# Selective scan of a two-layer vision block: two product buffers, one broadcast bank, two shared banks, and a hand-fixed VectorE order

## The chip, the cores and the metric

The kernel runs on one core of one Trainium2 chip. The metric is the device time of one execution in microseconds (us); of the kernel before there are three runs, and their median is the time to compare with. A core has five engines with an instruction stream each: TensorE (PE, matrix products; PEld is its weight load), VectorE (DVE), ScalarE (ACT), GpSimd (POOL) and SyncE (SP, which issues the DMAs here). Each engine works through its own stream in order, and waits on semaphores where it needs another engine's result. SBUF is the working memory, PSUM the memory that TensorE writes to.

## What is computed

The input is an image batch of 2 x 96 channels x 96 x 96. Two layers follow each other, each with a convolution-like part and a quantised feed-forward part. Only the first part of layer 0 matters here. Cut down, it is:

```python
xin, z = split(einsum(x, in_proj_w))            # 192 channels each; z = silu(z)
x_s    = grid_sample(xin, offsets(conv3x3(xin)))
# 6x6 = 36 tokens per sequence, 4 scan orders (rows, columns, both reversed)
x_dbl  = einsum(xs4, x_proj_weight)             # -> dts, Bs, Cs
delta  = softplus(dts + bias)
def step(h, (u, dt, b, c)):                     # 16 states per channel
    dA = exp(dt * A)
    h  = h * dA + (dt * u) * b                  # the scan
    y  = einsum(h, c)
y = sum of the four orders + D*u -> layer norm -> * z -> out_proj
```

So each of 192 channels has 16 states and four scan orders, and each state is a first-order recurrence along 36 tokens: `h = h * dA + (dt*u*b)`.

## The kernel before

**Tiling.** Layer 0 is cut into 32 stripes (2 images x 16 stripes of 6 rows, 576 tokens). Each stripe has three parts: a front (`_l0_front`: norm, projection, 3x3 convolution, sampling, B, C and the step sizes, stored to DRAM), the scan (`_l0_scan`) and a back (`_l0_back`: norm, gate, output projection, feed-forward). The front of stripe n+1 and the back of stripe n-1 run beside the scan of stripe n.

**A unit.** The scan of a stripe is 64 units: two halves `h` of the channels (32 units each), two token orders `o`, two directions `kk`, four quarters `i` of the states, two token halves `c`. One unit covers 128 partitions (32 channels x 4 states) and 3 blocks x 288 tokens = 864 elements. I count units from 0 to 63 within a stripe, and write for unit u:

- B(u): TensorE broadcasts the token's B to the partitions with one matmul into a PSUM bank (`spread`, L1040)
- p(u): VectorE multiplies it with `dur` into the PSUM tile `bp` (`product`, L1045; `bp` takes two banks)
- s(u): VectorE's scan from `dA` and `bp` into the SBUF tile `h` (L1060)
- t(u): GpSimd multiplies `h` with C in place (`times_c`, L1065)
- y(u): TensorE sums the states into the PSUM bank `y` (`states`, L1077); after it the `h` tile is free

`dA` is made on ScalarE, three instructions for two units (L1025), into two buffers; so the decay of units 2q and 2q+1 waits until s(2q-3) has read its buffer. There are six `h` tiles (`P.nh`). At the start of each half, six pairs of matmuls (`direct`, L966 and L968) put the D term into the bank `y`; they wait until ScalarE has copied the half before out of it (`out`, L976 and L978). `out` writes the tile `Y`, of which there is one: the next stripe's first half can leave only when the back of this one has read `Y` (its projection `pp`, L932 and L935, after GpSimd's gate, L921).

**PSUM.** Its 8 banks are dealt out as `y` one, `B` two, `bp` one tile of two banks, and three banks of the tag `p`, which all matmuls of the fronts and backs share.

**What sets the order.** The operations of all stripes are collected in a planner (`_Plan`). Each has an engine, a cost in us, tiles read and written and a due time. `order` simulates the engines: it starts next what can start first, and among what can start at once what is due first; across engines it adds a delay (`LAG`). A tile takes a slot of its tag when its first operation starts. The order found is then fixed for each engine, SP too (`_in_order`). The planner reckons with its own costs; the chip keeps the order, and waits where it must.

**Waits put ahead.** `wait` in `product` hangs extra waits on the products with c == 0: for the decays of this unit, and for t and y of unit u-5, if these were issued by then. The scan then has fewer waits of its own.

Of the kernel before, what the change touches and what calls it, by code (L numbers as in the profile page):

```python
# [13 lines left out]
ALU = mybir.AluOpType  # L14
# [14 lines left out]
WIN = 6  # L29
# [3 lines left out]
H2 = T // 2  # L33
NS = 16
KG = 4
NQ = 4
CB = 32
NBL = C // CB
# [50 lines left out]
class _Op:  # L89
    def __init__(self, eng, cost, run, due, tab):  # L90
        self.eng, self.cost, self.run, self.due, self.tab = eng, cost, run, due, tab
        self.deps, self.tiles, self.start, self.end = set(), [], None, None
        self.left, self.then, self.ready = 0, [], 0.0

SAME = 0.06
LAG = {"pe": 0.5, "dve": 1.5, "act": 0.6, "pool": 1.0, "sp": 1.5}


class _Plan:
# [39 lines left out]
    def order(self):  # L142

        free = {e: 0.0 for e in ("pe", "dve", "act", "pool", "sp")}
        ready = {e: [] for e in free}
        tab, wire = None, 0.0
        for n, o in enumerate(self.ops):
            o.no = n
            o.left = len(o.deps)
            for p in o.deps:  # L150
                p.then.append(o)
        for o in self.ops:
            if not o.left:
                ready[o.eng].append(o)
        left, out = {id(t): len(t.users) for o in self.ops for t in o.tiles}, []
        while len(out) < len(self.ops):
            best = None
            for e, queue in ready.items():
                pick = None
                for o in queue:  # L160
                    at = max(free[e], o.ready)
                    for t in o.tiles:
                        if t.slot is None:
                            s = t.place()
                            if s is None:
                                at = None
                                break
                            at = max(at, s[1] + (SAME if s[2] == e else LAG[e]))
                    if at is None:
                        continue  # L170
                    worth = o.due
                    if o.tab is not None and o.tab != tab:
                        worth += 5.0

                    key = (max(at, free[e] + 0.1), worth, o.no)
                    if pick is None or key < pick[0]:
                        pick = (key, at, o)
                if pick and (best is None or pick[1] < best[1]):
                    best = pick
            assert best, "the plan is stuck"  # L180
            _, at, o = best
            ready[o.eng].remove(o)
            cost = o.cost
            if o.tab is not None and o.tab != tab:
                tab, cost = o.tab, cost + 1.3
            for t in o.tiles:
                if t.slot is None:
                    t.slot = t.place()
                    t.slot[0] = t
                    if t.tag != "p":  # L190
                        t.queue.pop(0)
            o.start = at
            if o.eng == "sp":
                free["sp"] = at + 0.6
                wire = max(wire, at + 1.0) + cost
                o.end = wire + 2.0
            else:
                o.end = free[o.eng] = at + cost
            for p in o.then:
                p.left -= 1  # L200
                p.ready = max(p.ready, o.end + (SAME if p.eng == o.eng else LAG[p.eng]))
                if not p.left:
                    ready[p.eng].append(p)
            for t in o.tiles:
                left[id(t)] -= 1
                if o.end > t.slot[1]:
                    t.slot[1:] = o.end, o.eng
                if not left[id(t)]:
                    t.slot[0] = None
            out.append(o)  # L210
        return sorted(out, key=lambda o: (o.start, o.no))
# [739 lines left out]
def _l0_scan(k, P, S, n, f, tau):  # L951


    nc = k.nc
    f.Y = S.tile(P.hand, [C, 2, T], "Y", 1)
    for h in range(2):

        py = S.tile(P.ps, [128, 512], "y", 1)
        t0 = (64 * n + 32 * h) * tau

        def direct(h=h, py=py):

            for b in range(NBL):
                w = k.w_D[:, h, b * CB : b * CB + CB]
                v = f.xs0.ap[:, h]
                nc.tensor.matmul(py.ap[b * CB : b * CB + CB, :HEAD], w, v[:, :HEAD],  # L966
                                 start=True, stop=False)
                nc.tensor.matmul(_tail(py, b), w, v[:, HEAD:], start=b == 0, stop=False)  # L968

        S.op("pe", 1.4, direct, (f.xs0,), (py,), due=t0)  # L970
        for o in range(2):
            for kk in range(2):
                _l0_section(k, P, S, f, 64 * n + 32 * h, o, h, kk, py, t0 + (16 * o + 8 * kk) * tau, tau)

        def out(h=h, py=py):
            nc.scalar.copy(f.Y.ap[:, h, :HEAD], py.ap[:C, :HEAD])  # L976
            for b in range(NBL):
                nc.scalar.copy(f.Y.ap[b * CB : b * CB + CB, h, HEAD:], _tail(py, b))  # L978

        S.op("act", 1.4, out, (py,), (f.Y,), due=t0 + 33 * tau)  # L980
# [5 lines left out]
def _tail(py, b):  # L986

    n = T - HEAD
    return py.ap[NBL * CB :, b * n : b * n + n]


def _l0_section(k, P, S, f, first, o, h, kk, py, at, tau):
# [40 lines left out]

    def unit(u, i, c, cre, dA, t0):
        toks = slice(c * H2, (c + 1) * H2)
        pB, bp = S.tile(P.ps, [128, 512], "B", 2), S.tile(P.ps, [128, 1024], "bp", 1)
        ht = S.tile(P.rep, [128, NBL, H2], "h", P.nh)

        def spread():
            nc.tensor.matmul(  # L1040
                pB.ap[:, :H2], k.selb[:, kk, i, :], f.bc[o].ap[:, toks], start=True, stop=True)
            P.issued["B", u] = latest()

        def product():
            nc.vector.tensor_tensor(  # L1045
                bp.ap[:, : NBL * H2].rearrange("p (b n) -> p b n", b=NBL), dur.ap[:, :, toks],
                pB.ap[:, :H2].unsqueeze(1).to_broadcast([128, NBL, H2]), ALU.mult)
            if c == 0:
                free = u + 1 - P.nh
                wait([("act", u), ("B", u + 1), ("pool", free), ("pe", free)])  # L1050

        S.op("pe", 0.3, spread, (f.bc[o],), (pB,), due=t0 - P.early["pe"] * tau)
        S.op("dve", 1.13, product, (dur, pB), (bp,), due=t0 - P.early["dve"] * tau)

        def scan():
            hv, dv = (v.rearrange("p b n -> p (b n)") for v in (ht.ap, dA.ap[:, c]))
            bv = bp.ap[:, : NBL * H2]
            if kk:
                hv, dv, bv = hv[:, ::-1], dv[:, ::-1], bv[:, ::-1]
            nc.vector.tensor_tensor_scan(hv, dv, bv, 0.0, ALU.mult, ALU.add)  # L1060

        S.op("dve", 2.0, scan, (dA, bp), (ht,), due=t0 + (1.35 - P.early["dve"]) * tau)

        def times_c():
            nc.gpsimd.tensor_tensor(  # L1065
                ht.ap, ht.ap, cre.ap[:, toks].unsqueeze(1).to_broadcast([128, NBL, H2]), ALU.mult)
            P.issued["pool", u] = latest()

        S.op("pool", 2.06, times_c, (cre,), (ht,), due=t0 + (2.3 - P.early["pool"]) * tau)

        def states():
            end = o == 1 and kk == 1 and i == NQ - 1

            def part(dst, v, stop):
                if o:
                    v = v.rearrange("p (w j i) -> p w i j", i=WIN, j=WIN)
                nc.tensor.matmul(dst, k.fold, v, start=False, stop=stop)  # L1077

            for blk in range(NBL):
                dst = py.ap[CB * blk : CB * blk + CB]  # L1080
                n = HEAD - H2 if c else H2
                part(dst[:, c * H2 : c * H2 + n], ht.ap[:, blk, :n], end and c == 1)
            if c:
                for blk in range(NBL):
                    part(_tail(py, blk), ht.ap[:, blk, n:], end and blk == NBL - 1)
            P.issued["pe", u] = latest()

        S.op("pe", 1.0, states, (ht,), (py,), due=t0 + (3.5 - P.early["pe"]) * tau)

    for i in range(NQ):  # L1090
        quarter(i)
# [2 lines left out]
def _layer0(k, tc, a, x, x2d):  # L1094
# [3 lines left out]
    with ExitStack() as st:  # L1098
# [10 lines left out]
        P.ps = pool("ps0", 1, space=PSUM)  # L1109
        P.tc, P.issued = tc, {}  # L1110
        P.early = {"pe": 60, "act": 60, "dve": -30, "pool": 0, "sp": 8}
        P.np, P.ng, P.nda, P.nh = 3, 5, 2, 6
        start = len(nc.cur_bb.bb.instructions)
        S, tau = _Plan(k), 3.4
        stripes = [(b, s) for b in range(NB) for s in range(NW)]
        F = [Ctx() for _ in stripes]

# [831 lines left out]
```

## Time and profile before

| | us |
|---|---|
| median of 3 runs (8774.3 to 8780.41) | 8775.34 |
| span of the profiled execution | 8782.9 |
| first product to last scan | 146.8 to 6730.3 |
| 64 units of one stripe, mean | 205.7 |
| VectorE busy in 3000 to 3200 us | 190.93 of 200 |
| GpSimd busy in the same stretch | 181.78 of 200 |
| ScalarE busy in the same stretch | 149.30 of 200 |

The page gives busy time by engine and by groups of instructions; each group's row ends with the idle time of its engine just before it and what ended most of that. The scan stage is the stretch from 147 to 6730 us; layer 1 takes the rest. In the scan stage, a unit costs 6583.5 / 2048 = 3.21 us, of which VectorE's two instructions take 1.061 + 1.953 us.

### The profile page before, as it was taken

The page shows a single profiled execution, that of the slowest core. Times are in us where ns is not written, and L with a number is a line of the kernel's source. Part 1 is how long each engine was busy: PE and PEld are TensorE (multiplying, and loading weights), DVE is VectorE, ACT ScalarE, POOL GpSimd, SP SyncE. Part 2 cuts the span into 40 slices and gives each one's busy share as a digit, 9 for nine tenths or more (in the row PEclk, how much of TensorE's full clock was granted, in tenths as well). Part 3 has the DMA queues.
Part 4 walks back from the last instruction along what each step waited for, and adds up shares of the span by engine and source line. Part 5 has one row for each costly group of instructions (what it writes and reads, how often), then busy time and mean ns, then how long its engine had stood idle before and what let it go on. Part 6 is the DMA issues. An engine that isn't in the chain of part 4 may idle for free. (4 is left out here: it accounts for less than half of the span.)

```text
span 8782.9 us, 119686 instructions
## 1 busy us (share of the span) xinstructions
PE 7366.0 (84%) x43653; PEld 3436.2 (39%) x43653; DVE 8004.4 (91%) x5398; ACT 6381.2 (73%) x10720; POOL 6026.5 (69%) x3835
## 2 busy tenths in 40 slices
PE   7888888888888888888888888888865999989998
PEld 4333434434434343343343434334422323542245
DVE  3899999999999999999999999999997898959988
ACT  5677777777777777777777777777764787678867
POOL 4999998988899899898998888898885000010001
PEclk8898888998988888898888889888866999989999
DMA  2444444444444444444444444444442000110001
GB/s 85 139 149 144 145 145 141 146 143 141 142 141 145 137 151 144 142 142 146 145 142 143 142 143 138 145 139 142 142 140 87 19 2 9 34 51 2 3 21 32
DMA packets 339996, 985.64 MB, mean 112 GB/s; under 512 B 50152, under 2 KB 51872, under 8 KB 339104
## 3 DMA queue, kind: packets, MB, share of 16 engines
q1 hardware_dynamic: 337488, 977.74, 35.4%
q8 instruction: 346, 5.67, 0.3%
q14 instruction: 258, 2.11, 0.1%
q10 hardware_dynamic: 1904, 0.12, 0.0%
HBM read 797.19 MB, written 139.25 MB: 107 GB/s over the span
## 5 line engine op out<-in xcount | busy, mean ns | idle before, releaser
L1065 POOL TENSOR_TENSOR h<-h,cre 128x864 f32<-128x864 f32 x2048 | 4124.1, 2023 | 692.6 <-DVE h L1060 493.1
L1060 DVE TENSOR_TENSOR_SCAN h<-dA,bp 128x864 f32<-128x864 f32 x2048 | 3999.8, 1953 | 84.7 <-PE y L1077 6.3
L1025 ACT ACTIVATE dA<-dlr,A 128x576 f32<-128x576 f32 x3072 | 2156.4, 765 | 1098.8 <-DVE h L1060 1015.1
L1045 DVE TENSOR_TENSOR bp<-dur,B 128x864 f32<-128x864 f32 x2048 | 2172.9, 1061 | 295.9 <-PE B L1040 48.7
L1077 PE MATMUL y<-h,fold 128*32 128x288 f32 (+2 forms) x18432 | 1870.7, 452 | 161.6 <-POOL h L1065 152.0
L1040 PE MATMUL B<-bt,selb 128*128 128x288 bf16 x2048 | 642.4, 315 | 963.5 <-DVE bp L1045 951.1
L551 PE MATMUL pc<-xin,off 96*96 96x288 f32 x4608 | 1321.4, 414 | 0.5 <-ACT xin L516 0.4
L1077 PEld LDWEIGHTS y<-h,fold 128*32 128x32 f32 x18432 | 764.3, 119 | 1138.1 <-issue 548.9
L1413 ACT ACTIVATE pr<-sc 128x960 f32<-128x960 f32 (+1 forms) x1080 | 954.1, 937 | 200.3 <-PE sc L1409 180.3
L1493 DVE TENSOR_TENSOR sums<-sums,pr 128x3840 f32<-128x3840 f32 (+1 forms) x240 | 959.1, 3996 | 55.2 <-ACT pr L1413 33.2
L551 PEld LDWEIGHTS pc<-xin,off 96*96 96x96 f32 x4608 | 708.3, 165 | 514.3 <-issue 268.4
L1585 POOL MEMSET vch<- 96x32 f32 x16 | 2.4, 153 | 1296.6 <-DVE dist L1447 1209.3
L1040 PEld LDWEIGHTS <-selb 128*128 128x128 bf16 x2048 | 200.6, 99 | 1303.7 <-DVE bp L1045 797.9
L1409 PE MATMUL sc<-qH,kH 32*128 32x480 f32 (+1 forms) x3240 | 627.2, 602 | 9.7 <-issue 4.9
L1409 PE MATMUL sc<-q,kH 32*128 32x480 f32 (+1 forms) x1080 | 564.5, 602 | 0.0
L1475 PE MATMUL av<-pr,vT 128*32 128x480 f32 (+1 forms) x4320 | 532.6, 564 | 3.7 <-ACT av L1500 3.5
L1666 DVE SCALAR_TENSOR_TENSOR acc<-vch,lepe_w,acc 96x1152 f32<-96x1152 f32 x320 | 469.2, 1466 | 7.9
L867 POOL TENSOR_TENSOR x<-x,fy 96x576 f32<-96x576 f32 x32 | 56.1, 1755 | 480.6 <-ACT fy L866 400.6
L1409 PEld LDWEIGHTS sc<-qH,kH 32*128 32x128 f32 x3240 | 219.2, 184 | 418.3 <-issue 218.4
L724 PE MATMUL pt<-xd,w_dt 96*128 96x288 f32 x768 | 313.4, 500 | 26.4 <-ACT zs L534 14.8
L743 POOL TENSOR_TENSOR e<-e,du 128x576 f32<-128x576 f32 x192 | 271.6, 1414 | 31.5 <-ACT du L739 31.3
L745 POOL TENSOR_TENSOR dl<-dl,r 128x576 f32<-128x576 f32 x192 | 270.8, 1410 | 6.2
(270 smaller groups left out, 10159.0 us busy)
## 6 DMA issues: line engine op xcount, KB each, us to landing
cre<-c_d SPq DMA_DIRECT2D x1024, 288.0 KB
dur<-du_d SPq DMA_DIRECT2D x256, 864.0 KB
dlr<-dl_d SPq DMA_DIRECT2D x256, 864.0 KB
x<-xs SPq DMA_DIRECT2D x512, 72.0 KB
du_d<-du SPq DMA_DIRECT2D x128, 288.0 KB
dl_d<-dl SPq DMA_DIRECT2D x128, 288.0 KB
du_d<-du SPq DMA_DIRECT2D x128, 144.0 KB
dl_d<-dl SPq DMA_DIRECT2D x128, 144.0 KB
```

What stands on the lines that cost most here:

```text
L551: pe(H2, lambda: nc.tensor.matmul(pc.ap[:C, :H2], k.w_c1[:, ih, tap, oh * C : (oh + 1) * C], xin.ap[:, ih, 3 * c + dy : 3 * c + dy + 3, dx ...
L1025: nc.scalar.activation(dA.ap[:, :, blk, :], dlr.ap[:, blk, :].rearrange("p (c n) -> p c n", c=2), AF.Exp, scale=k.A[:, i, kg, h, blk : blk ...
L1040: nc.tensor.matmul(pB.ap[:, :H2], k.selb[:, kk, i, :], f.bc[o].ap[:, toks], start=True, stop=True)
L1045: nc.vector.tensor_tensor(bp.ap[:, : NBL * H2].rearrange("p (b n) -> p b n", b=NBL), dur.ap[:, :, toks], pB.ap[:, :H2].unsqueeze(1).to_bro ...
L1060: nc.vector.tensor_tensor_scan(hv, dv, bv, 0.0, ALU.mult, ALU.add)
L1065: nc.gpsimd.tensor_tensor(ht.ap, ht.ap, cre.ap[:, toks].unsqueeze(1).to_broadcast([128, NBL, H2]), ALU.mult)
L1077: nc.tensor.matmul(dst, k.fold, v, start=False, stop=stop)
L1409: nc.tensor.matmul(two[to // 2][:, to % 2, :n], kH[rows, k0 : k0 + 128], q, start=True, stop=True)
L1413: nc.scalar.activation(pr[:, 2 * i : 2 * i + 2, :n], two[i][:, :, :n], AF.Exp, scale=HD**-0.5)
L1475: nc.tensor.matmul((main if s < HEADS else other)[s * HD : (s + 1) * HD, :n], vT[:, blk, hd, :], pr[:, place(s, p), :n], start=at == 0, st ...
L1493: nc.vector.tensor_tensor(both, both, pr[:, :, :, :n], ALU.add)
L1666: S.op("dve", 1.43, lambda: nc.vector.scalar_tensor_tensor(acc.ap, src(), W.lw[:, t : t + 1], acc.ap, ALU.mult, ALU.add), (vch,), (acc,))
```

## The change

Four things change. The PSUM banks are dealt out anew: `B` one instead of two, `bp` two tiles instead of one (four banks), `p` two instead of three (`P.np`); `y` stays. VectorE's order of products and scans is fixed: both kinds of operation "write" a made-up tile `P.turn`, and the scan of a unit, with t and y, is handed to the planner only after the product of the next unit (`P.behind`), so that the order is p(1), s(0), p(2), s(1), and so on; at the end of each half `_l0_scan` hands in the last one, so that two scans and then two products stand together there. The planner's numbers change: product 1.13 to 1.0 and scan 2.0 to 1.9 us, and a matmul B is reckoned to VectorE's delay of 0.6 (`SOON`) instead of 1.5. The product no longer waits for the next unit's B.

```diff
-        self.left, self.then, self.ready = 0, [], 0.0
+        self.left, self.then, self.ready, self.lag = 0, [], 0.0, LAG
+SOON = {"dve": 0.6}
...
-                p.ready = max(p.ready, o.end + (SAME if p.eng == o.eng else LAG[p.eng]))
+                p.ready = max(p.ready, o.end + (SAME if p.eng == o.eng else o.lag[p.eng]))
...
+        P.behind()
+        P.behind = None
...
-        pB, bp = S.tile(P.ps, [128, 512], "B", 2), S.tile(P.ps, [128, 1024], "bp", 1)
+        pB, bp = S.tile(P.ps, [128, 512], "B", 1), S.tile(P.ps, [128, 1024], "bp", 2)
...
-                wait([("act", u), ("B", u + 1), ("pool", free), ("pe", free)])
+                wait([("act", u), ("pool", free), ("pe", free)])
...
-        S.op("pe", 0.3, spread, (f.bc[o],), (pB,), due=t0 - P.early["pe"] * tau)
-        S.op("dve", 1.13, product, (dur, pB), (bp,), due=t0 - P.early["dve"] * tau)
+        S.op("pe", 0.3, spread, (f.bc[o],), (pB,), due=t0 - P.early["pe"] * tau).lag = SOON
+        S.op("dve", 1.0, product, (dur, pB), (bp, P.turn), due=t0 - P.early["dve"] * tau)
...
-        S.op("dve", 2.0, scan, (dA, bp), (ht,), due=t0 + (1.35 - P.early["dve"]) * tau)
+        def rest():
...
+            S.op("dve", 1.9, scan, (dA, bp), (ht, P.turn), due=t0 + (1.35 - P.early["dve"]) * tau)
...
+        if P.behind:
+            P.behind()
+        P.behind = rest
...
-        P.np, P.ng, P.nda, P.nh = 3, 5, 2, 6
+        P.np, P.ng, P.nda, P.nh = 2, 5, 2, 6
...
+        P.turn, P.behind = S.held(k.ident, "turn"), None
```

More of the change, by code (lines that the diff above doesn't have):

```diff
@@ L1049, in product @@
                 free = u + 1 - P.nh
-                wait([("act", u), ("B", u + 1), ("pool", free), ("pe", free)])
-        S.op("pe", 0.3, spread, (f.bc[o],), (pB,), due=t0 - P.early["pe"] * tau)
-        S.op("dve", 1.13, product, (dur, pB), (bp,), due=t0 - P.early["dve"] * tau)
[L1055 to L1060, printed above, removed]
@@ L1062, in unit @@
-        S.op("dve", 2.0, scan, (dA, bp), (ht,), due=t0 + (1.35 - P.early["dve"]) * tau)
[L1064 to L1083, printed above, removed]
-                for blk in range(NBL):
-                    part(_tail(py, blk), ht.ap[:, blk, n:], end and blk == NBL - 1)
-            P.issued["pe", u] = latest()
@@ L1088, in unit, with scan, times_c, states @@
-        S.op("pe", 1.0, states, (ht,), (py,), due=t0 + (3.5 - P.early["pe"]) * tau)
+                wait([("act", u), ("pool", free), ("pe", free)])
+        S.op("pe", 0.3, spread, (f.bc[o],), (pB,), due=t0 - P.early["pe"] * tau).lag = SOON
+        S.op("dve", 1.0, product, (dur, pB), (bp, P.turn), due=t0 - P.early["dve"] * tau)
+        def rest():
+            def scan():
+                hv, dv = (v.rearrange("p b n -> p (b n)") for v in (ht.ap, dA.ap[:, c]))
+                bv = bp.ap[:, : NBL * H2]
+                if kk:
+                    hv, dv, bv = hv[:, ::-1], dv[:, ::-1], bv[:, ::-1]
+                nc.vector.tensor_tensor_scan(hv, dv, bv, 0.0, ALU.mult, ALU.add)
+            S.op("dve", 1.9, scan, (dA, bp), (ht, P.turn), due=t0 + (1.35 - P.early["dve"]) * tau)
+            def times_c():
+                nc.gpsimd.tensor_tensor(
+                    ht.ap, ht.ap, cre.ap[:, toks].unsqueeze(1).to_broadcast([128, NBL, H2]), ALU.mult)
+                P.issued["pool", u] = latest()
+            S.op("pool", 2.06, times_c, (cre,), (ht,), due=t0 + (2.3 - P.early["pool"]) * tau)
+            def states():
+                end = o == 1 and kk == 1 and i == NQ - 1
+                def part(dst, v, stop):
+                    if o:
+                        v = v.rearrange("p (w j i) -> p w i j", i=WIN, j=WIN)
+                    nc.tensor.matmul(dst, k.fold, v, start=False, stop=stop)
+                for blk in range(NBL):
+                    dst = py.ap[CB * blk : CB * blk + CB]
+                    n = HEAD - H2 if c else H2
+                    part(dst[:, c * H2 : c * H2 + n], ht.ap[:, blk, :n], end and c == 1)
+                if c:
+                    for blk in range(NBL):
+                        part(_tail(py, blk), ht.ap[:, blk, n:], end and blk == NBL - 1)
+                P.issued["pe", u] = latest()
+            S.op("pe", 1.0, states, (ht,), (py,), due=t0 + (3.5 - P.early["pe"]) * tau)
```

## The prediction

> **What bounds the kernel now.** I first read the windows of a stretch in mid-scan (columns: busy us of each engine), then the costliest groups of the page.
>
> ```profile
> 3000.00:3200.00 200.00, 164.43 (x970) 80.38 (x967) 190.93 (x132) 149.30 (x260) 181.78 (x114) 0.89 0.44 141
> ```
> ```profile
> L1065 POOL TENSOR_TENSOR h<-h,cre 128x864 f32<-128x864 f32 x2048 | 4124.1, 2023 | 692.6 <-DVE h L1060 493.1
> L1060 DVE TENSOR_TENSOR_SCAN h<-dA,bp 128x864 f32<-128x864 f32 x2048 | 3999.8, 1953 | 84.7 <-PE y L1077 6.3
> L1045 DVE TENSOR_TENSOR bp<-dur,B 128x864 f32<-128x864 f32 x2048 | 2172.9, 1061 | 295.9 <-PE B L1040 48.7
> ```
>
> VectorE is 95% busy and GpSimd 91%, so VectorE sets the pace, with little room on GpSimd. The idle time before scans and products, 85 + 296 us, is all that an order of VectorE can win. Its timeline shows what that idle time is made of:
>
> ```profile
> 3034.33 1.06 DVE L1045 TENSOR_TENSOR bp<-dur,B 128x864 f32<-128x864 f32 x1
> 3035.42 1.95 DVE L1060 TENSOR_TENSOR_SCAN h<-dA,bp 128x864 f32<-128x864 f32 x1
> 3037.51 1.06 DVE L1045 TENSOR_TENSOR bp<-dur,B 128x864 f32<-128x864 f32 x1
> ...
> 4090.46 1.95 DVE L1060 TENSOR_TENSOR_SCAN h<-dA,bp 128x864 f32<-128x864 f32 x1
> 4092.33 0.72 DVE L912 TENSOR_TENSOR Y<-Y,yva 96x576 f32<-96x576 f32 x1
> 4092.98 1.05 DVE L1045 TENSOR_TENSOR bp<-dur,B 128x864 f32<-128x864 f32 x1
> ```
>
> A scan that waits for the product just before it starts 0.03 to 0.04 us after its end; a product whose waits name several engines starts 0.14 us after the scan. An instruction that doesn't need its neighbour starts 0.08 us before the neighbour's end (4092.33 against 4090.46 + 1.95). Sorting all gaps by what the instruction waits for gives medians of 0.04 (VectorE alone), 0.11 (with TensorE), 0.14 (four engines), 0.23 (with a DMA) and -0.08 (neighbour not needed). These prices alone make 258 us; another 73 us are real stalls.
>
> What follows needs the half boundary too. The direct matmuls come after an idle TensorE at one pace, and after a busy one at another:
>
> ```profile
> 2425.62 1.05 PE L966 MATMUL y<-xs,w_D 96*32 96x504 f32 x1 [1.70 <-ACT Y L978]
> 2427.30 1.20 PE L1077 MATMUL y<-h,fold 128*32 128x288 f32 x6
> ...
> 2529.13 0.61 PE L966 MATMUL y<-xs,w_D 96*32 96x504 f32 x1 [0.88 <-ACT Y L978]
> 2530.00 1.79 PE L1077 MATMUL y<-h,fold 128*32 128x288 f32 x18
> ```
>
> Direct to y takes 1.68 or 0.87 us, one y 1.20 or about 0.6.
>
> **What the Trainium skill says.** "VectorE: DVE Perf Modes", The DRAIN you can't avoid, says that leaving out semaphores between chained operations saves nothing; its section on two Vector instructions with no wait lets one start earlier. The trace sides with the latter: 0.12 us between -0.08 and 0.04. "Perfetto Trace Analysis", Identifying Dependency Chains, says that an instruction waiting on several engines may get event-semaphore instructions ahead of it; the steps 0.04, 0.11, 0.14, 0.23 agree. "PSUM — Partial Sum Buffer", Specifications, gives 8 banks: all are dealt out before and after, so the second `bp` is paid with one `B` and one `p`.
>
> **The change part by part.** *VectorE's gaps.* The changed order has some 1,950 scans right behind a product they don't need: gap -0.08 instead of 0.036, from +76 to -156. Products still wait for the scan just before them (two tiles, and that scan reads the one they write), and now for TensorE too, as there is one `B`: 867 at 0.11 (95 us; before, 903 at 0.04), 737 at 0.14 (103), 255 at 0.23 (59), 125 beside another operation at -0.08 (-10). At each of the 64 half starts two products stand together; B(1) can only be written after p(0) ends: about 0.06 + 0.30 + 0.04 plus a matmul in between, 0.5 us, 32 us in all. Sum 116 to 123, against 258: -142 us.
>
> *B in one bank.* B(u) now has the length of s(u-2), 1.95 us, instead of that plus a unit. TensorE before was at B within 0.42 us of its bank coming free in three of four units, within 1.6 in nine of ten. The reckoned delay falls from 1.5 to 0.6, so it is placed sooner. Bounds: 0, or 0.095 us per unit (the mean excess over 1.6 us) = 195 us; I take it within the residual stalls below.
>
> *Two shared banks.* From the trace and the instruction order, a `p` bank is held by a matmul group until its last reader for 1.87 banks on average, three at once in 28% of the time (`pc` 19.0 us each, `pb` 12.9). 1.87 of 2 leaves nearly nothing, so the fronts and backs must run late, and the order shows it. The last `du` of a stripe's front stands on GpSimd 16 units ahead of that stripe's first t before, 0 units after; the back's gate stands 78 units after its stripe's start before, 96 after, which is exactly the half boundary where `out` needs `Y` back. GpSimd had at most 7 such instructions between two t's in steady state; now each stripe has two runs of 13. In 28 stripes the same three places repeat, where all six `h` tiles are full and TensorE has B(u) and front or back work queued ahead of the y that frees one:
>
> 1. Unit 6. TensorE: B(8), one `pc`, direct, y(0). B(8) waits for p(7); s(6), next on VectorE, waits for y(0). From the end of p(7): 0.2 (B) + 0.5 (`pc`, two passes of 0.243) + 0.87 to 1.68 + 0.6 to 1.20 + 0.1 = 2.3 to 3.7; I take 3.0.
> 2. Unit 38. TensorE: B(40), `pb` pair, five `pp`, direct, y(32); s(38) waits for y(32). With the end of s(37) at 0, p(39) ends at 1.2 and B(40) is through at 1.5. ScalarE's `dA` (2.11), released by s(37), stands ahead of the copy that frees a bank: free at 2.55. `pb` 1.24 to 3.8, `pp` 2.7 to 6.5, `out` on ScalarE 1.24 to 7.85, direct 1.68 to 9.6, y 1.2 to 10.8. s(38) could have started at 1.1: 9.7 us; without the bank's wait and with the quick paces 7.6. I take 9.3.
> 3. Unit 22. GpSimd runs 13 sampling and residual operations (17.8 us at 1.28 to 1.41) between t(15) and t(16). With the end of s(15) at 0: run ends at 19.9, p(23) at 20.0, B(24) 20.3. The last two `px` pairs need banks that ScalarE frees only after a `dA` (released at 18.9, done 21.05) and two copies (0.40 + 0.68): 22.1; pairs 1.1 each to 24.3 with the second bank at 22.9; y(16) 1.2: s(22) at 25.6 instead of 20.0: 5.6; bare 3.7. I take 5.2.
>
> Together 17.5 us x 29 stripes = 508 us. The waits ahead add a fourth: p(36) stands one scan sooner, 3.1 us instead of 6.2 after s(33), and ScalarE has 6.75 us of other work between the `dA`s released by s(31) and s(33): 6.75 + 2.11 - 6.3 = 2.6 late, done 4.7 after s(33), 1.5 us x 29 = 44. For all other products the wait for `dA` falls within 3.1 us in 86% of pairs by the times of before; bounds 0 and 0.118 x 1024 = 121 us. The stalls of before (73) lose most of their cause in the pauses: 40 left, with the two bounds above as room. First front and last back with two banks: +10.
>
> Sum on the profiled span: 8783 - 142 + (40 - 73) + 508 + 44 + 10 = 9170. The runs' median lies 8 us below the span: **9160**.
>
> **Rivals.** *It gains.* If the chip is far enough ahead of the planner (whose delay from VectorE is 1.5 us, while the trace has followers start 0.1 us after a scan), t and y come early and the `h` ring never fills: 8783 - 142 - 33 = 8608, so 8600. Against it: places 1 and 2 begin with a B that itself waits for the product just before the stalled scan, so no lead helps. It takes pauses below 6 us a stripe (175 / 29) for this side to win; even the bare lengths make 13.6.
> *Only the bare chains*, 13.6 x 29 = 394 and no wait ahead: 8783 - 142 - 73 + 394 = 8962, so 8955.
> *The banks bind further*: every `p` tile queues behind ScalarE's `dA`, B in one bank costs its 195 us and the decays 121: 9160 + 195 + 77 = 9430. Nothing in the order excludes it.
> *The change doesn't do what it says*: excluded, the order alternates p(u+1), s(u) but for the half boundaries and a few foreign operations.
>
> **How the numbers follow.** Forecast with its own spread 0.68; bare chains 0.13; banks bind further 0.12; gain 0.05, no change 0.02. The range runs from the bare chains to the bound banks: 8955 to 9430. Differences under 0.2%, 17 us, can't be told from none here. Faster 0.05, within 0.02, slower 0.93.
>
> **What would show it.** Scan groups with about -0.08 or no gap behind products; their idle sum moved to releasers "PE y" of some 400 to 550 us; in the timeline of VectorE three pauses a stripe, of 3, 5 and 9 us, at fixed units; ScalarE's and GpSimd's busy sums unchanged. I am wrong if the pauses are missing, if idle before products behind "PE B" exceeds 200 us in all units alike, or if VectorE's gaps behind products stay at 0.04.

## The result, and the profile after

The changed kernel takes 9295.96 us (median of 4 runs, 9291.97 to 9303.87) against 8776.67 us for the kernel before (now of 4 runs); the ratio is 1.0594, with a 95% interval of 1.0579 to 1.0609. It is 519 us slower; 9160 was forecast. The span of its profiled execution is 9294.8 us, 511.9 us more than before, and 503.8 us of these lie between the first product and the last scan (148.8 to 7236.1 us).

The window of mid-scan and the costliest groups of the page, the changed kernel:

```profile
3000.00:3200.00 200.00, 160.19 (x917) 80.41 (x916) 169.53 (x119) 143.95 (x241) 168.25 (x106) 0.87 0.42 133
```
```profile
L1069 POOL TENSOR_TENSOR h<-h,cre 128x864 f32<-128x864 f32 x2048 | 4104.7, 2020 | 1126.3 <-DVE h L1064 817.2
L1064 DVE TENSOR_TENSOR_SCAN h<-dA,bp 128x864 f32<-128x864 f32 x2048 | 3979.6, 1946 | 658.9 <-PE y L1081 643.0
L1048 DVE TENSOR_TENSOR bp<-dur,B 128x864 f32<-128x864 f32 x2048 | 2173.1, 1061 | 378.5 <-PE B L1043 105.8
```

VectorE and GpSimd both lost ground, 169.53 and 168.25 busy of 200, so neither is the bound any more. The scans' idle time went from 84.7 to 658.9 us, and y ends 643.0 of it. (Lines moved: the scan is L1064, the product L1048, B L1043, y L1081, t L1069.)

The timeline of VectorE shows both sides of the change, first in undisturbed units and then at unit 38 of stripe 15:

```profile
3565.15 1.95 DVE L1064 TENSOR_TENSOR_SCAN h<-dA,bp 128x864 f32<-128x864 f32 x1
3567.23 1.06 DVE L1048 TENSOR_TENSOR bp<-dur,B 128x864 f32<-128x864 f32 x1
3568.20 1.95 DVE L1064 TENSOR_TENSOR_SCAN h<-dA,bp 128x864 f32<-128x864 f32 x1
...
3601.05 1.06 DVE L1048 TENSOR_TENSOR bp<-dur,B 128x864 f32<-128x864 f32 x1
3615.18 1.95 DVE L1064 TENSOR_TENSOR_SCAN h<-dA,bp 128x864 f32<-128x864 f32 x1 [13.07 <-PE y L1081]
```

The scan at 3568.20 starts 0.09 us before the product's end (3567.23 + 1.06): the gap is gone, as the change meant. At 3615.18 a scan has waited 13.07 us. All gaps of the scan stage before a product or scan, added up by size, give the whole account (a gap is negative where the next instruction starts before the end of the one ahead):

| us | before | after | difference |
|---|---|---|---|
| gaps up to 0.3 us before scans | 70.2 | -173.2 | -243.4 |
| gaps up to 0.3 us before products | 170.6 | 195.7 | +25.1 |
| longer, before scans of units 6, 22 and 38 | 0.9 | 623.9 | +623.0 |
| longer, all others | 80.5 | 194.6 | +114.1 |
| scans' duration (1953 and 1946 ns x 2048) | 3999.7 | 3985.4 | -14.3 |

The sum is +504.5, against 503.8 measured. So the short gaps gave the gain that the order was made for, 218 us, and three fixed places of each stripe took nearly three times as much.

### The profile page after: what moved, and what is told of

The parts are those of the page before. It is cut to its first block, busy times and chain, and to the rows that moved or that the text cites. A ratio compares the mean times of both kernels' runs of the same rounds, so it can differ in the third digit from the quotient of the medians.

```text
span 9294.8 us, 120737 instructions
## 1 busy us (share of the span) xinstructions
PE 7644.1 (82%) x43653; PEld 3599.9 (39%) x43653; DVE 7812.5 (84%) x5398; ACT 6524.9 (70%) x10824; POOL 6055.7 (65%) x3835
## 5 line engine op out<-in xcount | busy, mean ns | idle before, releaser
L1069 POOL TENSOR_TENSOR h<-h,cre 128x864 f32<-128x864 f32 x2048 | 4104.7, 2020 | 1126.3 <-DVE h L1064 817.2
L1064 DVE TENSOR_TENSOR_SCAN h<-dA,bp 128x864 f32<-128x864 f32 x2048 | 3979.6, 1946 | 658.9 <-PE y L1081 643.0
L1048 DVE TENSOR_TENSOR bp<-dur,B 128x864 f32<-128x864 f32 x2048 | 2173.1, 1061 | 378.5 <-PE B L1043 105.8
L1081 PE MATMUL y<-h,fold 128*32 128x288 f32 (+2 forms) x18432 | 1862.2, 459 | 159.2 <-POOL h L1069 155.9
L1043 PE MATMUL B<-bt,selb 128*128 128x288 bf16 x2048 | 666.0, 325 | 1034.1 <-DVE bp L1048 1025.4
L552 PE MATMUL pc<-xin,off 96*96 96x288 f32 x4608 | 1276.5, 410 | 0.5 <-ACT xin L517 0.4
L1081 PEld LDWEIGHTS y<-h,fold 128*32 128x32 f32 x18432 | 788.4, 120 | 1170.6 <-POOL h L1069 639.5
L1043 PEld LDWEIGHTS <-selb 128*128 128x128 bf16 x2048 | 209.3, 102 | 846.1 <-issue 780.5
L725 PE MATMUL pt<-xd,w_dt 96*128 96x288 f32 x768 | 336.2, 534 | 71.1 <-DVE xn L509 31.6
L730 ACT ACTIVATE e<-pt,dt_b 128x288 f32<-128x288 f32 x384 | 189.2, 493 | 171.1 <-PE pt L725 169.5
```

The source lines that it names most:

```text
L552: pe(H2, lambda: nc.tensor.matmul(pc.ap[:C, :H2], k.w_c1[:, ih, tap, oh * C : (oh + 1) * C], xin.ap[:, ih, 3 * c + dy : 3 * c + dy + 3, dx ...
L1043: nc.tensor.matmul(pB.ap[:, :H2], k.selb[:, kk, i, :], f.bc[o].ap[:, toks], start=True, stop=True)
L1048: nc.vector.tensor_tensor(bp.ap[:, : NBL * H2].rearrange("p (b n) -> p b n", b=NBL), dur.ap[:, :, toks], pB.ap[:, :H2].unsqueeze(1).to_bro ...
L1069: nc.gpsimd.tensor_tensor(ht.ap, ht.ap, cre.ap[:, toks].unsqueeze(1).to_broadcast([128, NBL, H2]), ALU.mult)
```

## The experiments

Two theories stood against each other. Theory A: the two shared banks `p` make fronts and backs late, so that the six `h` tiles fill at fixed places. Theory B: the fixed order or the single `B` bank costs the time.

**Two shared banks alone**, on the kernel before:

```diff
-        P.np, P.ng, P.nda, P.nh = 3, 5, 2, 6
+        P.np, P.ng, P.nda, P.nh = 2, 5, 2, 6
```

> The kernel before with two shared banks p instead of three, nothing else. Theory A (the two shared banks make fronts and backs late, so that the six h tiles fill at fixed places of a stripe): 9150 to 9450 us, with pauses of several us on VectorE at a few fixed units. Theory B (the fixed VectorE order and the single B bank cost the time): 8760 to 8830 us, no such pauses.

9154.34 us, ratio 1.0429 (1.0399 to 1.0460), +377 us. Its groups:

```profile
L1060 DVE TENSOR_TENSOR_SCAN h<-dA,bp 128x864 f32<-128x864 f32 x2048 | 3999.9, 1953 | 371.5 <-PE y L1077 283.9
L1045 DVE TENSOR_TENSOR bp<-dur,B 128x864 f32<-128x864 f32 x2048 | 2173.5, 1061 | 284.2 <-PE B L1040 53.2
```

The products' idle time stayed where it was (295.9 before), the scans' rose by 287 us and is ended by y: the sign of the result, from one bank less. The places are other ones: units 6, 14 and 36, with 6.5, 7.2 and 4.1 us each, in 12 to 14 stripes. (Another 51 us of idle time came before VectorE's product of the back, L912.) Nothing but the number of shared banks and the order that the planner makes of it differs here, so this run speaks for theory A.

**One B bank alone**, on the kernel before:

```diff
-        pB, bp = S.tile(P.ps, [128, 512], "B", 2), S.tile(P.ps, [128, 1024], "bp", 1)
+        pB, bp = S.tile(P.ps, [128, 512], "B", 1), S.tile(P.ps, [128, 1024], "bp", 1)
```

> The kernel before with one B bank instead of two, nothing else (a PSUM bank stays unused). Theory A: within 50 us of before, so 8730 to 8830. Theory B: 9000 us or more, with idle time before the products ended by the B matmul of 200 us or more.

8972.04 us, ratio 1.0222 (1.0189 to 1.0255), +194 us (166 to 224 by the interval). Theory A expected no change and missed. Theory B missed its number of 9000, but the idle time before products ended by the matmul of `B` is 212.8 us, as it said. One B bank is a cost of its own when the planner is left as it was.

**One B bank with the shorter reckoned delay** (with the lines of the change that make `SOON` work). In `_Plan.order` the delay is chosen by the engine that waits, so `SOON` shortens the reckoned time from B's end to its product; it doesn't place B sooner after the product before it, as I had read it.

```diff
-        S.op("pe", 0.3, spread, (f.bc[o],), (pB,), due=t0 - P.early["pe"] * tau)
+        S.op("pe", 0.3, spread, (f.bc[o],), (pB,), due=t0 - P.early["pe"] * tau).lag = SOON
```

> The kernel before with one B bank and the shorter reckoned delay from B to the product. If the 195 us that one B bank cost alone came from the planner's long delay (B placed late or the products ordered around it): 8780 to 8850 us. If they came from the bank itself (B can only be written after the product before it has ended): 8930 us or more.

8919.93 us, ratio 1.0162 (1.0133 to 1.0192), +143 us: between the two expectations, nearer the second. The delay accounts for some 51 of the 194 us, the bank and the order that goes with it for the rest; the two intervals (117 to 169 and 166 to 224 us) just touch, so the split is rough. The idle time of products ended by `B` fell from 212.8 to 113.9 us.

**The changed banks without the second bp and the fixed order** (two `p`, one `B`, the shorter delay with the lines that make it work, one `bp`, the planner's own order):

```diff
-        P.np, P.ng, P.nda, P.nh = 3, 5, 2, 6
+        P.np, P.ng, P.nda, P.nh = 2, 5, 2, 6
...
-        pB, bp = S.tile(P.ps, [128, 512], "B", 2), S.tile(P.ps, [128, 1024], "bp", 1)
+        pB, bp = S.tile(P.ps, [128, 512], "B", 1), S.tile(P.ps, [128, 1024], "bp", 1)
...
-        S.op("pe", 0.3, spread, (f.bc[o],), (pB,), due=t0 - P.early["pe"] * tau)
+        S.op("pe", 0.3, spread, (f.bc[o],), (pB,), due=t0 - P.early["pe"] * tau).lag = SOON
```

> The kernel before with two shared banks, one B bank and the shorter reckoned delay from B to the product, but one bp and VectorE's order left to the planner: the changed kernel without its second bp and its fixed order. Theory A (the shared banks carry the loss; the order gains about 200 us by its gaps): 9400 to 9600 us, more than the changed kernel's 9296. Theory B (the fixed order carries a part of the loss): below 9250 us.

9492.88 us, ratio 1.0815 (1.0784 to 1.0846), in theory A's range. With it the change comes apart into steps: two `p` alone +377, one `B` with the shorter delay alone +143, both together +716, and the second `bp` with the order, its costs and without the wait for the next `B` on top, 9296 - 9493 = -197 us. Together the two shortages cost more than apart (716 against 520 for the sum); no run tells whether the banks do this or the order that the planner then finds. The second `bp` with the fixed order is a gain.

**The fixed order taken off the changed kernel**, with both `bp` kept:

```diff
-        P.behind()
-        P.behind = None
...
-        S.op("dve", 1.0, product, (dur, pB), (bp, P.turn), due=t0 - P.early["dve"] * tau)
+        S.op("dve", 1.0, product, (dur, pB), (bp,), due=t0 - P.early["dve"] * tau)
...
-            S.op("dve", 1.9, scan, (dA, bp), (ht, P.turn), due=t0 + (1.35 - P.early["dve"]) * tau)
+            S.op("dve", 1.9, scan, (dA, bp), (ht,), due=t0 + (1.35 - P.early["dve"]) * tau)
...
-        if P.behind:
-            P.behind()
-        P.behind = rest
+        rest()
```

> The changed kernel's banks and numbers, with the order of products and scans left to the planner. Theory A: pauses of the same kind and size or more, and gaps of 0.035 us where a scan follows its own product: 9300 to 9700 us. Theory B (the fixed order itself costs): below 9200 us.

9470.83 us, ratio 1.0790 (1.0758 to 1.0821). The fixed order is no cause of the loss; without it the kernel is 175 us slower still. Two `bp` without the order differ by 22 us from the run above, which is within the two intervals.

**Less load on the shared banks.** A third `p` bank can't be had beside two `bp`: `y`, `B`, four for `bp` and three make nine of eight. So I took load off instead. The convolution's matmul group `pc` holds a shared bank 19.0 us; here seven of its nine taps are left out, in the kernel before and in the changed one:

```diff
-            for tap in range(9):
+            for tap in (0, 8):
```

> The kernel before with 2 of the 9 convolution taps of layer 0 (it leaves out seven taps, 14 of the 18 matmuls of each pc group, so that a pc group holds its shared bank far shorter). VectorE's work is unchanged, so both theories: 8650 to 8790 us.

> The changed kernel with the same seven taps left out. Theory A (the two shared banks are too few for the fronts' and backs' holding times): with some 60 us less of holding per stripe the pauses mostly go, 8550 to 8800 us, and the idle time before scans ended by y falls from 643 to under 200 us. Theory B (the order and the single B bank): the loss stays, 9150 us or more.

8745.48 us on the kernel before, 8836.48 us on the changed one, ratios to the full kernel before 0.9954 (0.9938 to 0.9970) and 1.0067 (1.0044 to 1.0090). The loss fell from 519 to 91 us. The scans' idle time is 20.7 us (15.4 ended by y), so the three pauses are gone; but the products' is 597.2 us, 268.6 of it ended by B. A part of the stall moved from y to the matmul of `B`: theory A was right on the pauses and missed the time by 36 us. In both runs TensorE's mean granted clock is 0.80, against 0.89 and 0.86 with all taps, so its other matmuls are not at the same pace.

**And the feed-forward of layer 0 left out too**, in both:

```diff
-    x2 = _plan_ffn(k, S, op, ps, temp, P.back, 1, ffn, x1)
+    x2 = x1
```

> The kernel before with seven of nine taps and the feed-forward of layer 0 left out. VectorE loses the 64 small fxq products (27 us); both theories: 8600 to 8780 us.

> The changed kernel with the same taps and feed-forward left out: the shared banks are held least here. Theory A: faster than its counterpart b_both by 100 to 220 us, since only the shorter gaps behind products are left (218 us by the trace of the changed kernel). Theory B: slower than b_both by 300 us or more.

8712.66 us and 8597.56 us: with the shared banks least loaded, the changed order is 115 us faster than its counterpart (ratios to the full kernel before 0.9923, 0.9894 to 0.9952, and 0.9792, 0.9764 to 0.9820). The groups of VectorE, first the order before, then the changed one:

```profile
L1060 DVE TENSOR_TENSOR_SCAN h<-dA,bp 128x864 f32<-128x864 f32 x2048 | 3998.3, 1952 | 83.8 <-ACT dA L1025 7.6
L1045 DVE TENSOR_TENSOR bp<-dur,B 128x864 f32<-128x864 f32 x2048 | 2174.3, 1062 | 275.5 <-DVE h L1060 45.1
```
```profile
L1064 DVE TENSOR_TENSOR_SCAN h<-dA,bp 128x864 f32<-128x864 f32 x2048 | 3978.5, 1945 | 42.7 <-PE y L1081 38.0
L1048 DVE TENSOR_TENSOR bp<-dur,B 128x864 f32<-128x864 f32 x2048 | 2173.3, 1061 | 368.3 <-PE B L1043 87.5
```

No scan group has the 659 us any more. The gaps up to 0.3 us sum to 24.8 us against 245.1, the same 220 us of gain as in the full kernel; stalls of 182 us against 62 give about half of it back. So of theory B the fixed order is excluded as a cause, and the single `B` bank is not: the same order with the same bank is a gain here, but alone the bank cost 143 to 194 us. These two pairs take load off TensorE, ScalarE and GpSimd as well as off the shared banks; by themselves they don't tell one from the other. That the banks matter is shown by the run with two shared banks alone, which changes no engine's work.

**bp in SBUF.** The other way to three shared banks is to move `bp` out of PSUM, with fewer tiles of two other tags to make room:

```diff
-        cre, dA = S.tile(P.rep, [128, T], "cre", 4), S.tile(P.rep, [128, 2, NBL, H2], "dA", P.nda)
+        cre, dA = S.tile(P.rep, [128, T], "cre", 3), S.tile(P.rep, [128, 2, NBL, H2], "dA", P.nda)
...
-        pB, bp = S.tile(P.ps, [128, 512], "B", 1), S.tile(P.ps, [128, 1024], "bp", 2)
+        pB, bp = S.tile(P.ps, [128, 512], "B", 1), S.tile(P.rep, [128, NBL * H2], "bp", 2)
...
-        P.np, P.ng, P.nda, P.nh = 2, 5, 2, 6
+        P.np, P.ng, P.nda, P.nh = 3, 4, 2, 6
```

> The changed kernel with both bp tiles in SBUF, which leaves room for three shared banks p again (B stays one bank, VectorE's order stays fixed); to make room in SBUF there are four g tiles instead of five and three cre tiles instead of four. Theory A: the pauses at units 6, 22 and 38 shrink to under 2 us each, and with the shorter gaps behind products the time is 8550 to 8750 us, if product and scan keep 1.06 and 1.95 us with bp in SBUF. Theory B: 9200 to 9350 us.

11670.57 us, ratio 1.3296 (1.3257 to 1.3335): the condition of the expectation failed, so this run says nothing on the banks.

```profile
L1069 POOL TENSOR_TENSOR h<-h,cre 128x864 f32<-128x864 f32 x2048 | 5246.9, 2580 | 1154.6 <-DVE h L1064 885.9
L1064 DVE TENSOR_TENSOR_SCAN h<-dA,bp 128x864 f32<-128x864 f32 x2048 | 5820.1, 2844 | 263.2 <-PE y L1081 203.3
```

The scan takes 2.84 us instead of 1.95 and GpSimd's t 2.58 instead of 2.02, while the product, which still reads B from PSUM, keeps 1.05. The Trainium skill, "SBUF — State Buffer", section SBUF: two separate sides, says that a VectorE operation with two SBUF inputs and a GpSimd operation lock one pair of ports against each other. The scan has two SBUF inputs only here, and both partners grew. The durations within this run agree with the page: 114 scans start while GpSimd runs no TENSOR_TENSOR operation, and take 1.95 us (median); the 1,934 that start while it runs one have a median of 2.80. And t takes 3.66 us (median) in the 940 cases where it starts during a scan, 2.02 in the others.

**Moving the order around the shortage.** In the changed kernel, once the due time of the direct matmuls was put ahead by TensorE's lead, once those of the fronts were put about 20 units ahead:

```diff
-        S.op("pe", 1.4, direct, (f.xs0,), (py,), due=t0)
+        S.op("pe", 1.4, direct, (f.xs0,), (py,), due=t0 - P.early["pe"] * tau)
```
```diff
-            t0, t1 = (64 * n - 90) * tau, (64 * n - 12) * tau
+            t0, t1 = (64 * n - 110) * tau, (64 * n - 30) * tau
```

> The changed kernel with the due time of the direct matmuls moved ahead by 60 units, so that the planner puts them before the convolution. Theory A: the pause at unit 6 (77 us in all) goes, the one at unit 38 (333 us) stays within 60 us since there the direct matmuls wait for the projection; 9190 to 9260 us. If the direct matmuls' place were the cause of both: 8900 to 9000 us.

> The changed kernel with the due times of the fronts 20 units and 18 units sooner (nothing else). The order shows that no direct then stands behind a B at unit 8 with a pc in between, but the second half's still stands behind B(40) and the projection. Theory A: some pauses move and the loss shrinks by 50 to 250 us, to 9050 to 9250, without going: the bank shortage stays. If the phase of the fronts were the cause: within 100 us of before.

With direct first: 9605.95 us, ratio 1.0944 (1.0847 to 1.1041), outside both ranges. The pause at unit 6 went, as expected, but the one at unit 38 grew from 11 to 19 us a stripe (569 us in all): its queue ahead of direct now holds more of the back: `yva`, `pt`, `pd` and `pb` groups and both `pp`. A new pause of 129 us in all came at unit 25, and 225 us of idle time before the back's product L913 (13.6 in the changed kernel). I had expected unit 38 to stay; here one moved due time moved the other places too. With the fronts early: 9110.47 us, ratio 1.0379 (1.0349 to 1.0409), in the expected range; units 6 and 22 are no longer among the long pauses, unit 38 still costs 327 us.

No version that does the whole work beats the kernel before. Whether the fixed order would with nine banks wasn't tried, as there are eight.

## Why the prediction was right, and where its sum was off

**VectorE's gaps.** Forecast -142 with the half starts at +32, so -174 for the prices alone; measured -218 and +35.5. (-142 takes the lower end of "116 to 123"; the terms listed there add up to 123.) Of the 258 us of before the table finds 241, as the forecast's prices were rounded up. After the change, scans were put at -156 and came to -173, since the scan after a product it doesn't need starts 0.091 before the product's end and not 0.08; products were put at 240 and came to 196. A part of that is bookkeeping: 251 products, 73 before, have longer gaps and are counted with the stalls. The waits kept their prices: 0.104 for products that wait for VectorE and TensorE, 0.133 for four engines, 0.231 with a DMA.

**The three pauses** are where the order of instructions put them, and of the size of their chains: unit 6 77 us in all (2.7 each, forecast 3.0), unit 22 214 (7.6, forecast 5.2), unit 38 333 (11.1, forecast 9.3). Forecast 508, measured 624. The chain at unit 38 of stripe 15, TensorE's timeline of the changed kernel:

```profile
3599.33 1.17 PE L933 MATMUL pp<-xr,ident 96*96 96x288 f32 x2
3600.30 2.13 PE L936 MATMUL pp<-zs,w_outb 96*96 96x288 f32 x4
3602.21 2.13 PE L936 MATMUL pp<-Y,out_proj 96*96 96x288 f32 x4
3604.27 0.42 PE L673 MATMUL pb<-bt,minus 32*32 32x288 bf16 x1
3604.62 0.42 PE L1043 MATMUL B<-bt,selb 128*128 128x288 bf16 x1
3605.17 2.29 PE L661 MATMUL pb<-xs,w_bc 96*128 96x288 f32 x4
3607.25 1.16 PE L933 MATMUL pp<-xr,ident 96*96 96x288 f32 x2
3608.21 2.12 PE L936 MATMUL pp<-zs,w_outb 96*96 96x288 f32 x4
3610.13 2.00 PE L936 MATMUL pp<-Y,out_proj 96*96 96x288 f32 x4
3612.06 0.31 PE L673 MATMUL pb<-bt,minus 64*64 64x288 bf16 x1
3613.52 0.61 PE L967 MATMUL y<-xs,w_D 96*32 96x504 f32 x1 [1.15 <-ACT Y L981]
...
3614.39 0.86 PE L1081 MATMUL y<-h,fold 128*32 128x288 f32 x15
```

and `out` on ScalarE in the same place:

```profile
3607.49 0.40 ACT L668 CAST bt<-pb 128x288 bf16<-128x288 f32 x1 [1.95 <-PE pb L661]
3607.90 0.39 ACT L669 COPY rest<-pb 32x288 f32<-32x288 f32 x1
3612.22 0.57 ACT L979 COPY Y<-y 96x504 f32<-96x504 f32 x1 [3.93 <-PE pp L936]
3612.81 0.66 ACT L981 COPY Y<-y 32x72 f32<-32x72 f32 x3
```

B, `pb`, `pp`, `out`, direct, y, then the scan at 3615.18: these are the links that the prediction drew, in its order. The term that was mis-sized is the matmuls' pace, in two of the links. `pb` and `pp` take 6.9 us here (3605.17 to 3612.06) and not 1.24 + 2.7 = 3.9. And B(40), put at 0.3 us from the end of p(39) to its own, starts 2.5 us after that end (3604.62 against 3602.11), because it stands behind an earlier `pp` group; in 26 of 30 stripes it starts 1.3 us or more late. The wait for a bank, put at 1 us, is 0.1 here, and direct takes 0.87 us to y and not 1.68.

The pace can be checked against the granted clock. Two windows of the changed kernel (us, busy us of PE, PEld, DVE, ACT and POOL, then the granted clock), the first in this stripe, the second the pause at unit 38 of stripe 14 up to just after direct's start:

```profile
3598.22:3611.88 13.66, 12.67 (x28) 6.93 (x27) 3.79 (x3) 4.22 (x9) 13.23 (x11) 0.50 0.74 230
3382.73:3390.00 7.27, 5.87 (x26) 3.29 (x28) 0.00 (x0) 3.88 (x11) 7.08 (x7) 0.97 0.80 248
```

In stripe 14 `pb` and `pp` take 3.6 us, and the pause is 8.8 us. Over all stripes the pause at unit 38 goes with the clock: seven of 8.8 to 8.9 us at 0.97 to 0.98, four of 9.8 at 0.83, six of 11.8 to 11.9 at 0.64 to 0.69, eleven of 13.0 to 13.2 at 0.63 (stripes 1 and 2 are irregular). At full pace the forecast's 7.6 to 9.7 us hold; by this an estimated 76 of the 333 us are the slower clock. The 28 pauses at unit 22 all lie at a clock of 0.50 to 0.60 (a `px` pair took 2.0 us and not 1.1), those at unit 6 at 1.00.

The pause doesn't bring the half pace (a granted clock of 0.50) on: it was granted from 3598.22 on, and the pause begins at 3602.11. The Trainium skill, "TensorE: Matmul & The Clock Gate", What's actually happening, says that the clock halves after an idle window of some 3.4 us and returns after as long a busy one. This trace doesn't agree: in the 3.4 us before 3598.22 TensorE was busy for 1.55 us, and the half pace then lasted 13.66 us, of which it was busy for 12.67. What sets the clock here stays open.

**The wait ahead at p(36)**, forecast at 44 us, didn't come: it isn't among the pauses. Delays before products at units 25, 26, 48 and 52, which weren't foreseen, make 81 us together. That the one roughly made up for the other in the total is luck.

**One B bank** was left within the residual stalls, with its bound of 195 us. Alone it cost 194, near the bound by chance as far as the runs show, since a part of that was the planner's delay. In the changed kernel the idle time ended by `B` is 105.8 us against 48.7; that the pauses swallow the rest is likely, but not shown. Two reasons of that paragraph were wrong: `SOON` shortens the delay to the product, and the planner's 1.5 us belong to VectorE as the one that waits. Neither carried a number of the sum.

**The sum.** Terms as forecast against measured: prices -174 and -218, half starts +32 and +35.5, the pauses +508 and +623, all other stalls +11 (44 less 33) and +79, the scans' duration 0 and -14, start and end +10 and +8. That is +387 against +513 (511.9 on the span). Sign, places and links of the loss were forecast for the right reason; its size was a quarter short, by the pauses' pace and the stalls, and an underrated gain of 44 us hid a part of that. The forecast of two shared banks as the main cause is borne out by the run with these alone (+377); which units the shortage hits depends on the order that the planner finds.

## What to carry to other kernels

Before buffers are dealt out anew in a full PSUM, add up how long each tag's banks are held, from the first write to the last read; here 1.87 of 3 were held on average, and taking one away cost 377 us, more than the 218 us that the tighter order won on the bounding engine. Find where a ring (here six tiles) can fill: look in each engine's order for the instruction that frees a slot, and for what stands ahead of it in that queue. A chain that begins with a wait on the stalled engine itself can't be hidden by a lead of the other engines; summed over all stripes, such chains give a low estimate of the loss of that order (forecast 394 us bare, measured 624). And look up the granted clock at those places before giving their matmuls a duration.

## What the runs showed of the hardware

An instruction of VectorE that needs nothing from the one before it starts 0.08 to 0.09 us before that one's end; one that does starts 0.035 us after it. Over the 1,925 scans of the changed kernel without a longer wait that is about 240 us. The scan itself is 7 ns shorter behind a product that it doesn't wait for (1946 against 1953 ns); in the run without the fixed order, which has both kinds, it is 1946 ns in 459 scans and 1954 in 1,280. A scan with both inputs in SBUF takes 1.95 us (median) where GpSimd runs no TENSOR_TENSOR operation at its start, and 2.80 where it does. And TensorE's granted clock stayed at 0.50 for 13.66 us in which TensorE was busy for 12.67.
